# Second attention: the queries of two heads in seven products of blocks, and the groups of one batch element after those of the other

## The chip, the cores and the metric

The kernel runs on one core of a Trainium2 chip. The time is the device time of one execution, in microseconds (us). A run before the change took 2154.76 us, the median of three (2153.85 to 2155.38).

Five engines work side by side, each through its own instructions in order: PE (matrix products; its weight loads are listed apart as PEld), DVE (vector work), ACT (activations and copies), POOL (vector work out of SBUF) and SP, which issues the DMAs.

## The reference, cut to what matters

The program is a chain of six blocks on x of 2 x 512 tokens by 512 features, all in float32. The second one is the attention that the change touches: 32 query heads of 128 features, 8 key heads, so four query heads share one group of keys and values.

```python
q = (hidden_states @ Wq.T).reshape(bsz, q_len, N_HEADS, HEAD_DIM).transpose(0, 2, 1, 3)
...
q = q * cos + _rotate_half(q) * sin
k = k * cos + _rotate_half(k) * sin
...
c_kv = hidden_states @ Wdk.T
k_c = c_kv @ Wupk.T
v = (c_kv @ Wupv.T).reshape(bsz, q_len, KV_HEADS, HEAD_DIM).transpose(0, 2, 1, 3)
...
scores = jnp.einsum('bhqd,bhkd->bhqk', q, k) * scale
scores = jnp.where(causal[None, None], scores, jnp.asarray(-1000000000.0, dt))
attn = jax.nn.softmax(scores, axis=-1)
out = jnp.einsum('bhqk,bhkd->bhqd', attn, v)
...
return out @ Wo.T
```

`hidden_states` is the layernorm of x, and the result is added to x. For one head the query product is 512 tokens x 512 features x 128 outputs.

## The kernel before

**Layout.** `k.xT[b]` holds the normalised x of batch element b, transposed: features on the partitions, four chunks of 128, by 512 tokens (the tokens in an order in which two of the four tiles run backwards). It is a part of the tile `room`, of which two more parts, `k.spare`, take the probabilities of two units in turn. PSUM's eight banks of 512 columns are held for the whole block and handed out in rotation by `k.turn()`.

**Groups and units.** Before, `groups` runs over the 8 groups and inside a group over the two batch elements: 16 pairs (g, b). A unit is one head of one pair: 64 units. The weights of a group (`wq`, `wo`, `wk`, `wupv`, by `load`, L685) are loaded once and serve both elements; `wq` and `wo` are tiles of 1 MB with the tag w8, which has five buffers and is shared with `wdk` and with the weights of `bound`, a side computation on POOL that a later block needs.

**The start.** L693 to L704 make the latents `ckvT` of both elements: four chains of four products each. The layernorm of the second element's tokens (L698) stands between the two.

**The loop** (L821 to L828), written out by hand, sets PE's order; the planner of the framework orders the other engines by its costs and priorities. In step n:
- `queries` of unit n+1 (L753): a chain of four 128x512 products over the four chunks of features into one bank; then `rope` (L706), three DVE operations out of PSUM (the product with the cosine, and two halves with the sine) and one add on POOL.
- `softmax` of unit n (L760): `exponents` (L222) makes the scores of four query tiles, each in four strips of 32 columns of PE, then DVE adds the mask and takes the maxima, and ACT makes the exponentials with their sums; `normalise` (L259) has a reciprocal on DVE and four products on POOL.
- `beside` (L783), by the place j of the unit in its group. j = 0: the fourth output chain of the group before the last. j = 1: `values` of the last group, 64 products on PE (`attend`), with copies by ACT (`gather`). j = 2: `prepare_keys` of the next group, and two output chains of the last. j = 3: `prepare_values` of the next group, with 16 small DMAs (`spread`, L322), and one output chain.
- `turned` of unit n-1 (L273): DVE transposes the probabilities in blocks of 32 for `values`.

At the end of the block (m = 16, L800) stands the layernorm of the first element for the next block.

Of the kernel before, what the change touches and what calls it, by code (L numbers as in the profile page):

```python
# [31 lines left out]
F32 = mybir.dt.float32  # L32
I32 = mybir.dt.int32
AF = mybir.ActivationFunctionType
ALU = mybir.AluOpType
AX = mybir.AxisListType

B, S, D = 2, 512, 512
P = 128
NT = S // P  # L40
KC = D // P
NTILES = B * NT
# [3 lines left out]
class Block:  # L46
# [39 lines left out]
    def masks(self):  # L86
        nc = self.nc


        self.mask = self.const.tile([P, S], F32, tag="mask", name="mask")  # L90
        nc.gpsimd.memset(self.mask, 0.0)
        nc.gpsimd.affine_select(
            out=self.mask, in_=self.mask, compare_op=ALU.is_ge, fill=-1e30, base=S - P,
            pattern=[[-1, S]], channel_multiplier=1,
        )

        self.mask_back = self.const.tile([P, S], F32, tag="mask_back", name="mask_back")
        nc.gpsimd.memset(self.mask_back, 0.0)
        back = self.mask_back[:, :P]
        nc.gpsimd.affine_select(  # L100
            out=back, in_=back, compare_op=ALU.is_ge, fill=-1e30, base=0,
            pattern=[[1, P]], channel_multiplier=-1,
        )


    def load(self, src, shape, tag, bufs=None, dtype=F32, pool=None):
# [564 lines left out]
def attn_gqa(k, a, bound):  # L671


    nc, tc = k.nc, k.tc
    G, J = 8, 4
    with ExitStack() as ctx:
        lp = ctx.enter_context(tc.tile_pool(name="b", bufs=2))
        one = lambda shape, tag: lp.tile(shape, F32, tag=tag, name=tag, bufs=1)
        wdk = k.load(a["b_wdk"], [P, KC, D], "w8", 5)
        tables = {}  # L680
        for n in ("cosq", "sinq", "cosk", "sink"):
            tables[n] = one([P, S], n)
            nc.sync.dma_start(out=tables[n], in_=a["c_b_" + n])

        def load(g):  # L685
            return dict(
                wq=k.load(a["b_wq"][g], [P, KC, J * P], "w8", 5),
                wo=k.load(a["b_wo"][g], [P, J, D], "w8", 5),
                wk=k.load(a["b_wk"][g], [P, KC, P], "w3", 6),
                wupv=k.load(a["b_wupv"][g], [P, KC, P], "w3", 6),  # L690
            )

        w = {0: load(0)}  # L693
        ckvT = []
        for b in range(B):
            if b:
                for t in range(NT, NTILES):
                    k.layernorm(t, k.turn, back=True)  # L698
            ck = one([P, KC, S], f"ckvT{b}")
            for m in range(KC):  # L700
                ps = k.turn()
                k.chain(ps, [(wdk[:, c, bass.ts(m, P)], k.xT[b][:, c]) for c in range(KC)])
                nc.scalar.copy(ck[:, m], ps)
            ckvT.append(ck)  # L704

        def rope(ps, kind, out):  # L706

            cos, sin = tables["cos" + kind], tables["sin" + kind]
            t2 = k.work.tile([P, S], F32, tag="xn", name="t2")
            nc.vector.tensor_tensor(out, ps, cos, ALU.mult)  # L710
            nc.vector.tensor_tensor(t2[0:64], ps[64:128], sin[64:128], ALU.mult)
            nc.vector.tensor_tensor(t2[64:128], ps[0:64], sin[0:64], ALU.mult)  # L712
            nc.gpsimd.tensor_tensor(out, out, t2, ALU.add)  # L713

        keys, vals = {}, {}

        def prepare_keys(g, b):

            ps = k.turn()


            for c in range(KC):
                for n in range(4):
                    strip = slice(32 * n, 32 * n + 32)
                    src = ckvT[b] if n % 2 else k.xT[b]
                    nc.tensor.matmul(
                        ps[strip],
                        w[g]["wk"][:, c, strip],
                        src[:, c],
                        start=(c == 0),  # L730
                        stop=(c == KC - 1),
                    )
            kt = lp.tile([P, S], F32, tag="kT", name="kT", bufs=3)
            rope(ps, "k", kt)
            keys[g, b] = kt

        def prepare_values(g, b):

            ps = k.turn()
            for t in range(NT):  # L740
                k.chain(
                    ps[:, bass.ts(t, P)],
                    [(ckvT[b][:, c, bass.ts(t, P)], w[g]["wupv"][:, c]) for c in range(KC)],
                )
            vt = lp.tile([P, NT, P], F32, tag="v", name="v")
            nc.scalar.copy(vt.rearrange("p t d -> p (t d)"), ps)
            vals[g, b] = lp.tile([P, S // 32, P], F32, tag="vals", name="vals")
            k.spread(vt, vals[g, b])

        qs, ctxs = {}, {}  # L750
        turned = one([P, J * k.WIDE], "turned")

        def queries(u):  # L753
            g, b, j = u
            ps = k.turn()
            k.chain(ps, [(w[g]["wq"][:, c, bass.ts(j, P)], k.xT[b][:, c]) for c in range(KC)])
            q = qs[u] = lp.tile([P, S], F32, tag="q", name="q")
            rope(ps, "q", q)

        def softmax(u):  # L760
            g, b, j = u
            q = qs.pop(u)
            probs = k.other().rearrange("p t s -> p (t s)")
            k.normalise(probs, k.exponents(q, keys[g, b], probs))
            return probs

        def values(g, b):
            banks = [k.turn() for i in range(4)]
            v = vals[g, b]
            k.attend(banks, [(slice(0, P), lambda i, n: v[32 * i : 32 * i + 32, n], turned)])  # L770
            c = ctxs[g, b] = lp.tile([P, J, S], F32, tag="ctxT", name="ctxT", bufs=1)
            k.gather(banks, c, [nc.scalar.copy] * 4)

        def output(g, b, t):
            ps = k.turn()
            c = ctxs[g, b]
            k.chain(ps, [(c[:, i, bass.ts(t, P)], w[g]["wo"][:, i]) for i in range(J)])
            k.add_to_x(b * NT + t, ps)

        groups = [(g, b) for g in range(G) for b in range(B)]  # L780
        units = [(g, b, j) for g, b in groups for j in range(J)]

        def beside(m, j):  # L783


            before = groups[m - 1] if 0 < m <= len(groups) else None
            if before and j == 1:
                values(*before)
            if m < len(groups) and j == 2 and m + 1 < len(groups):
                prepare_keys(*groups[m + 1])  # L790
            if before and j == 2:
                output(*before, 0)
                output(*before, 1)
            if j == 3 and m + 1 < len(groups):
                prepare_values(*groups[m + 1])
            if before and j == 3:
                output(*before, 2)
            if m > 1 and j == 0:
                output(*groups[m - 2], 3)
            if m == len(groups) and j in (1, 2):  # L800

                for t in (2 * j - 2, 2 * j - 1):
                    k.layernorm(t, k.turn)
            if m < len(groups) and groups[m][1] == 1 and j == 1 and groups[m][0] + 1 < G:
                w[groups[m][0] + 1] = load(groups[m][0] + 1)
            for at, n in ((4, "q"), (9, "k")):
                if (m, j) == (at, 2):
                    bound.begin(n)
                if m == at + 1:
                    bound.square(j)  # L810
                if (m, j) == (at + 2, 0):
                    bound.sum()
            if (m, j) == (12, 0):
                bound.end()

        with tc.manual_schedule(engines={mybir.EngineType.PE}):
            prepare_keys(0, 0)
            queries(units[0])
            prepare_values(0, 0)
            probs = {}  # L820
            for n in range(len(units) + J + 1):  # L821
                if n + 1 < len(units):
                    queries(units[n + 1])
                if n < len(units):
                    probs[n] = softmax(units[n])
                beside(*divmod(n, J))
                if n - 1 in probs:
                    k.turned(probs.pop(n - 1), turned, (n - 1) % J)  # L828

# [813 lines left out]
```

## Time and profile before

| what | value | how to read it |
|---|---|---|
| median of the runs | 2154.76 us | three runs |
| the profiled execution | 2156.43 us | its own time |
| span in its trace | 2154.7 us | first to last instruction |
| mean granted PE clock | 0.987 | over the whole span |
| second attention | about 344 to 1180 us | from the first latent's chain to the last group's values |
| DVE query cosine, 128x512 out of PSUM | 692 ns | L710 |
| POOL query add, 128x512 | 1283 ns, x64 | L713 |
| POOL products of `normalise` | 372, 478, 585, 692 ns | 128, 256, 384, 512 columns, L265 |
| load of `wq` or `wo` | 1 MB, 4.8 us from issue to landing | x8 each |
| load of `vals` by `spread` | 64 KB, 2.0 us | x256 |

A row of the profile gives the source line, the engine, the operation, the tiles written and read, the count, the busy time and the mean time of one. "Idle before" is time in which the engine stood still ahead of these instructions, put down to what ended it. A PE record's time is longer than its share of the stream, since records overlap; the distance between starts is what a product costs.

### The profile page before, as it was taken

What the parts mean: (1) busy time and instruction counts of PE and PEld (TensorE: products, weight loads), DVE (VectorE), ACT (ScalarE), POOL (GpSimd) and SP (SyncE); (2) the same over time, 40 slices, a digit from 0 to 9 for tenths busy, and PEclk for the clock granted to TensorE, in tenths of its full rate; (3) what the DMA queues carried; (4) which work ended last, traced back from release to release, by engine and by line L of the source; (5) the groups of instructions that cost most, each with busy time, mean ns of one, the idle gap of its engine ahead of it and who ended that gap; (6) DMA issues with size and microseconds to landing.
All of it is one profiled execution on the core that took longest, in us unless ns stands there. A gap on an engine that the chain in (4) does not pass through costs nothing. (4 is left out here: it accounts for less than half of the span.)

```text
span 2154.7 us, 38870 instructions
## 1 busy us (share of the span) xinstructions
PE 2068.3 (96%) x15116; PEld 1085.4 (50%) x15116; DVE 1281.2 (59%) x3467; ACT 728.8 (34%) x2040; POOL 719.2 (33%) x988
## 2 busy tenths in 40 slices
PE   7999989999999999999999989999999989999988
PEld 3444434555555555555555444545454544554554
DVE  6578752655555555555555557666666674745745
ACT  2455531222222222222222145444545211532531
POOL 1101010423323324223223246555555544215220
PEclk9999999999999999999999999999999999999999
DMA  3000021211121212121110321010101002002001
GB/s 97 16 1 1 20 89 41 68 40 50 40 70 41 68 25 69 26 84 30 46 36 10 126 60 53 21 51 23 49 22 51 1 30 44 2 2 40 1 2 40
DMA packets 65463, 85.35 MB, mean 40 GB/s; under 512 B 13170, under 2 KB 50162, under 8 KB 60660
## 3 DMA queue, kind: packets, MB, share of 16 engines
q1 hardware_dynamic: 64628, 81.69, 12.7%
q8 instruction: 123, 2.02, 0.4%
q10 hardware_dynamic: 640, 1.05, 0.3%
q14 instruction: 72, 0.59, 0.1%
HBM read 58.59 MB, written 2.10 MB: 28 GB/s over the span
## 5 line engine op out<-in xcount | busy, mean ns | idle before, releaser
L254 ACT ACTIVATE room<-room,nmax 128x128 f32<-128x128 f32 (+3 forms) x384 | 211.2, 551 | 507.3 <-DVE nmax L244 506.2
L265 POOL TENSOR_SCALAR room<-room,invs 128x128 f32<-128x128 f32 (+3 forms) x384 | 197.0, 532 | 95.9 <-DVE invs L262 95.9
L713 POOL TENSOR_TENSOR q<-q,t 128x512 f32<-128x512 f32 x64 | 82.1, 1283 | 423.4 <-DVE t L712 423.4
L305 PE MATMUL sc<-turned,vals 32*128 32x256 f32 (+7 forms) x1004 | 187.3, 420 | 0.0
L305 PE MATMUL tp<-turned,vals 32*128 32x384 f32 (+7 forms) x742 | 170.9, 411 | 0.0
L305 PE MATMUL pj<-turned,vals 32*128 32x384 f32 (+7 forms) x754 | 146.8, 416 | 3.1 <-DVE turned L278 3.1
L233 PE MATMUL sc<-kT,q 128*32 128x160 f32 (+15 forms) x1536 | 139.5, 399 | 8.6 <-DVE invs L262 7.9
L278 DVE STREAM_TRANSPOSE turned<-room 128x1152 f32<-128x1152 f32 x80 | 108.0, 1363 | 66.4 <-POOL room L265 22.1
L305 PEld LDWEIGHTS sc<-turned,vals 32*128 32x128 f32 (+1 forms) x1004 | 122.5, 167 | 6.2 <-issue 4.1
L160 PE MATMUL pj<-room,w 128*128 128x512 f32 x272 | 121.1, 595 | 0.2 <-ACT room L191 0.2
L160 PE MATMUL sc<-room,w 128*128 128x512 f32 x232 | 105.4, 597 | 0.2 <-ACT room L191 0.2
L305 PEld LDWEIGHTS tp<-turned,vals 32*128 32x128 f32 (+1 forms) x742 | 102.9, 167 | 5.0 <-issue 2.7
L305 PEld LDWEIGHTS pj<-turned,vals 32*128 32x128 f32 (+1 forms) x754 | 97.8, 169 | 11.8 <-DVE turned L278 5.8
L160 PE MATMUL sc<-w,room 128*128 128x512 f32 (+1 forms) x224 | 100.5, 595 | 0.0
L233 PE MATMUL tp<-kT,q 128*32 128x224 f32 (+15 forms) x1032 | 92.4, 392 | 6.9 <-DVE invs L262 6.9
L201 POOL TENSOR_TENSOR rstd<-ve,mhalf 128x1 f32<-128x1 f32 x80 | 44.1, 554 | 160.8 <-DVE ve L199 137.4
L233 PE MATMUL pj<-kT,q 128*32 128x512 f32 (+4 forms) x992 | 92.7, 407 | 2.9 <-POOL q L993 1.9
L254 ACT ACTIVATE probs<-probs,nmax 128x128 f32<-128x128 f32 (+3 forms) x128 | 71.1, 556 | 65.5 <-DVE nmax L244 64.2
L160 PE MATMUL sc<-w,ctxT 128*128 128x512 f32 x192 | 87.5, 598 | 0.0
L233 PEld LDWEIGHTS sc<-kT,q 128*32 128x32 f32 x1536 | 61.8, 110 | 50.0 <-issue 20.6
L265 POOL TENSOR_SCALAR probs<-probs,invs 128x128 f32<-128x128 f32 (+3 forms) x128 | 65.6, 532 | 61.3 <-DVE invs L262 57.4
L523 PE MATMUL sc<-qm,keys 32*128 32x512 f32 x198 | 85.5, 638 | 0.0
(577 smaller groups left out, 5734.6 us busy)
## 6 DMA issues: line engine op xcount, KB each, us to landing
vals<-v SPq DMA_DIRECT2D x256, 64.0 KB, 2.0
w<-in_b_wq SPq DMA_DIRECT2D x8, 1024.0 KB, 4.8
w<-in_b_wo SPq DMA_DIRECT2D x8, 1024.0 KB, 4.8
w<-in_m_wo SPq DMA_DIRECT2D x8, 1024.0 KB, 6.4
w<-in_f_w SPq DMA_DIRECT2D x4, 1024.0 KB, 4.8
w<-in_m_wqn SPq DMA_DIRECT2D x8, 384.0 KB, 3.2
x<-in_x SPq DMA_DIRECT2D x8, 256.0 KB, 5.1
w<-in_b_wk SPq DMA_DIRECT2D x8, 256.0 KB, 2.6
```

Source lines behind the costliest of these rows:

```text
L160: last = self.nc.tensor.matmul(out, lhsT, rhs, start=(i == 0), stop=(i == len(pairs) - 1))
L201: self.nc.gpsimd.tensor_tensor(r, ve, self.mhalf, ALU.pow)
L233: nc.tensor.matmul(ps[32 * i : 32 * i + 32, a - lo : b - lo], q[:, at : at + 32], keys[:, a:b], start=True, stop=True,)
L254: nc.scalar.activation(row, row, AF.Exp, bias=nmax, scale=-1.0, accum_out=total[:, qt : qt + 1])
L265: self.nc.gpsimd.tensor_scalar(row, row, inv[:, qt : qt + 1], 1.0, ALU.mult, ALU.mult)
L278: self.nc.vector.transpose(out[:, :last], probs[:, :last])
L305: self.nc.tensor.matmul(out[:, :, :n], values(i, j), rhs, start=(j == blocks[0]), stop=(j == stop[i]),)
L523: nc.tensor.matmul(ps, keys[b][rows[g], bass.ts(kc, P)], qm[u][rows[g]], start=True, stop=True)
L713: nc.gpsimd.tensor_tensor(out, out, t2, ALU.add)
```

## The change

**Seven products.** Two heads and the two halves of the features make weight blocks a11, a12 (first head), a21, a22 (second); the halves of the features and of the tokens make the blocks of x. In place of eight products of blocks (each now 128 outputs x 256 tokens, two chunks of features), seven are made, of sums of blocks:
- `token_sums(b)`: four DVE subtractions (128x512 elements), once per batch element.
- `weight_sums(m, i)`: four POOL operations (128x256) for each pair of heads, one of which overwrites a21 in the weight tile.
- `queries(m, i, part)`: part 0 makes two products, which ACT copies out of PSUM; part 1 two more, with two DVE adds and two POOL adds; part 2 the last three, with three DVE adds, then the rotation: two DVE halves with the sine for each head, now out of SBUF, and the product with the cosine and the add on POOL.

In the loop, a pair's parts 0 and 1 stand around the scores of an even unit, and part 2 ahead of the scores of the odd one; they are for the pair of the next two units.

**The order of the groups.** All eight groups of the first element, then all of the second. Each of the 16 groups loads its own `wq`, `wo`, `wk` and `wupv`, and `wdk` is loaded a second time (at m = 5). The second element's layernorm (m = 5) and latents (m = 7, j = 0 and 1) move from the start into the loop, and the first element's layernorm for the next block from the end to m = 13. `ckvT` has one buffer, `kT` two in place of three, `v` one in place of two, `q` three in place of two.

**The masks** of two tiles of 512 columns become two views of one tile of 640.

```diff
         def load(g):
             return dict(
                 wq=k.load(a["b_wq"][g], [P, KC, J * P], "w8", 5),
-                wo=k.load(a["b_wo"][g], [P, J, D], "w8", 5),
...
+        groups = [(g, b) for b in range(B) for g in range(G)]
...
+        tokens = lambda b, c, n: k.xT[b][:, 2 * c : 2 * c + 2, bass.ts(n, S // 2)]
+        heads = lambda m, i, r, c: w[m]["wq"][:, 2 * c : 2 * c + 2, bass.ts(2 * i + r, P)]
+
+        ends = [s.rearrange("p c s -> p (c s)")[:, k.TRIANGLE :] for s in k.spare]
+        xs = [one([P, 2, S // 2], f"x_sum{i}") for i in range(3)]
+        xs.append(ends[1][:, :S].rearrange("p (c s) -> p c s", c=2))
...
+        def token_sums(b):
+            sub = lambda out, x, y: nc.vector.tensor_tensor(out, x, y, ALU.subtract)
+            sub(xs[0], tokens(b, 0, 1), tokens(b, 0, 0))
+            sub(xs[1], tokens(b, 1, 1), xs[0])
+            sub(xs[2], tokens(b, 1, 1), tokens(b, 0, 1))
+            sub(xs[3], tokens(b, 1, 0), xs[1])
+
+        def weight_sums(m, i):
+            op = nc.gpsimd.tensor_tensor
+            s = lp.tile([P, 3, 2, P], F32, tag="wq_sum", name="wq_sum")
+            both, less, last = (s[:, n] for n in range(3))
+            a11, a12, a21, a22 = (heads(m, i, r, c) for r in range(2) for c in range(2))
+            op(both, a21, a22, ALU.add)
+            op(less, both, a11, ALU.subtract)
+            op(last, a12, less, ALU.subtract)
+            op(a21, a11, a21, ALU.subtract)
+            ws[m, i] = a11, a12, a21, a22, both, less, last
+
+        def product(out, lhsT, rhs):
+            for c in range(2):
+                nc.tensor.matmul(out, lhsT[:, c], rhs[:, c], start=c == 0, stop=c == 1)
...
-        def queries(u):
-            g, b, j = u
-            ps = k.turn()
-            k.chain(ps, [(w[g]["wq"][:, c, bass.ts(j, P)], k.xT[b][:, c]) for c in range(KC)])
-            q = qs[u] = lp.tile([P, S], F32, tag="q", name="q")
-            rope(ps, "q", q)
+        def queries(m, i, part):
...
+            if part == 0:
+                ps = k.turn()
+                product(ps[:, first], a11, x(0, 0))
+                product(ps[:, second], both, xs[0])
+                nc.scalar.copy(copies, ps)
+            elif part == 1:
...
+                ps = k.turn()
+                product(ps[:, first], less, xs[1])
+                product(ps[:, second], diff, xs[2])
+                add(q0[:, second], ps[:, first], copies[:, first])
+                add(q1[:, first], ps[:, second], q0[:, second])
+                for out, of in ((q0[:, second], q0[:, second]), (q1[:, second], q1[:, first])):
+                    nc.gpsimd.tensor_tensor(out, of, copies[:, second], ALU.add)
+            else:
...
+                product(ps[:, first], a12, x(1, 0))
+                product(ps[:, second], a22, xs[3])
+                add(q0[:, first], ps[:, first], copies[:, first])
+                add(q1[:, first], ps[:, second], q1[:, first])
+                ps = k.turn()
+                product(ps[:, first], last, x(1, 1))
+                add(q0[:, second], ps[:, first], q0[:, second])
+                for q in pair:
...
+                    nc.vector.tensor_tensor(t2[0:64], q[64:128], sin[64:128], ALU.mult)
+                    nc.vector.tensor_tensor(t2[64:128], q[0:64], sin[0:64], ALU.mult)
+                    nc.gpsimd.tensor_tensor(q, q, tables["cosq"], ALU.mult)
+                    nc.gpsimd.tensor_tensor(q, q, t2, ALU.add)
...
             for n in range(len(units) + J + 1):
-                if n + 1 < len(units):
-                    queries(units[n + 1])
+                m, i = divmod((n + 2) // 2, 2)
+                more = m < len(groups)
+                if more:
+                    queries(m, i, 2 * (n % 2))
                 if n < len(units):
-                    probs[n] = softmax(units[n])
+                    probs[n] = softmax(*units[n])
+                if more and n % 2 == 0:
+                    queries(m, i, 1)
+                if (m, i, n % 2) == (G - 1, 1, 1):
+                    token_sums(1)
                 beside(*divmod(n, J))
+                if n % 2 == 0 and n + 4 < len(units):
+                    weight_sums(*divmod(n // 2 + 2, 2))
                 if n - 1 in probs:
                     k.turned(probs.pop(n - 1), turned, (n - 1) % J)
```

## The prediction

> **What bounds the kernel.** I read the page's busy shares and slices first, then the busy time by windows inside the second attention, then the waits there, then single weight loads on the time line. The page's own chain of waits is short here (PE 7% of the span) and says nothing of this stage.
>
> ```profile
> PE 2068.3 (96%) x15116; PEld 1085.4 (50%) x15116; DVE 1281.2 (59%) x3467; ACT 728.8 (34%) x2040; POOL 719.2 (33%) x988
> ...
> PE   7999989999999999999999989999999989999988
> ...
> POOL 1101010423323324223223246555555544215220
> PEclk9999999999999999999999999999999999999999
> ```
> ```profile
> 600.00:700.00 100.00, 100.00 (x740) 55.16 (x739) 51.76 (x125) 24.10 (x82) 27.27 (x40) 1.00 0.19 56
> 700.00:800.00 100.00, 100.00 (x739) 55.88 (x741) 52.96 (x123) 23.88 (x81) 27.88 (x40) 1.00 0.17 48
> ```
> The windows' columns are PE, PEld, DVE, ACT, POOL, then granted clock. From 380 to 1150 us PE is never idle at a granted clock of 1.00, DVE is at 53%, POOL at 27 to 39%. The stage is bound by PE's stream, so PE work removed there is time removed, as long as nothing else becomes late. The waits of the stage say the same: the long ones are of other engines for PE's products.
>
> ```profile
> ACT room L254 <- DVE nmax L244: 486.7, 61, 13.6
> POOL q L713 <- DVE t L712: 407.0, 61, 9.1
> ```
>
> **PE: the products.** PE's price is read from the starts of the weight loads.
> ```profile
> 382.07 3.54 PEld L160 LDWEIGHTS pj<-w,ckvT 128*128 128x128 f32 x31 [0.24 <-issue]
> 385.53 0.30 PEld L160 LDWEIGHTS tp<-room,w 128*128 128x128 f32 x2
> 386.08 0.19 PEld L160 LDWEIGHTS tp<-room,w 128*128 128x128 f32 x1 [0.24 <-issue]
> 386.51 0.19 PEld L160 LDWEIGHTS tp<-room,w 128*128 128x128 f32 x1 [0.24 <-issue]
> ...
> 388.22 0.19 PEld L160 LDWEIGHTS tp<-room,w 128*128 128x128 f32 x1 [0.24 <-issue]
> 389.17 0.16 PEld L233 LDWEIGHTS sc<-kT,q 128*32 128x32 f32 x8 [0.76 <-issue]
> ```
> Each fp32 matmul of the program is two records (four of a query chain give eight loads). With 512 columns a record takes 0.429 us (386.08 to 386.51). With 128 columns, 32 records take 385.53 - 382.07 = 3.46 us, 0.108 each: a quarter, so even there the loads of 128 weights stay hidden. A record of 256 columns, which the trace lacks, is then 0.214 us (between a half, 0.214, and 0.22 with the small surplus of the 128-column row). Two heads cost 16 x 0.429 = 6.86 us; seven products of two matmuls are 28 records x 0.214 = 6.00. Gain 0.86 us a pair, x32 pairs = **-27.4 us** (-22 with 0.22).
>
> **PE: one more change of tiling per group.** In step j=2 the keys followed the scores at once, both with 32-column weights; now the products of part 1 stand between.
> ```profile
> 540.25 0.53 PEld L233 LDWEIGHTS sc<-kT,q 128*32 128x32 f32 x8
> 540.92 0.11 PEld L726 LDWEIGHTS av<-room,w 128*32 128x32 f32 x1
> ...
> 544.89 0.30 PEld L160 LDWEIGHTS sc<-w,ctxT 128*128 128x128 f32 x2 [0.84 <-ACT room L254]
> 545.42 0.19 PEld L160 LDWEIGHTS sc<-w,ctxT 128*128 128x128 f32 x1 [0.24 <-issue]
> ```
> Into 32-column weights costs 0.09 us (the matmul loaded at 388.22 ends at 389.08, the next load is at 389.17). Out of them costs 0.22: the last keys end at 544.78, the first full matmul starts at 545.42 - 0.43 = 544.99. Together 0.31 x 15 groups with keys after scores = **+4.7 us**. The other steps keep their number of changes.
>
> **DVE and ACT.** Per pair DVE loses two cosine products (0.69 each) and gains five adds of 256 columns from PSUM (no row; nearest, the masked maximum of 128x256, 0.42): 2.1 - 1.4 = +0.7 us in 23 us, on an engine at 53%. ACT gains one copy of 512 columns, 0.59, at 24%. Beside PE, 0. They come ahead of the scores' maxima in DVE's queue, which the next scores' banks wait for: eight banks in rotation are about 11 us of PE work, so that cover is wide.
>
> **POOL** takes most. A two-input 128x512 takes 1.28 us; 256 columns I estimate at 0.7 (half, plus part of a fixed cost of about 0.27, from the scaling rows 0.48 at 256 and 0.69 at 512). Per group of four heads: sums of weights 8 x 0.7 = 5.6, part 1's adds 4 x 0.7 = 2.8, cosine product and last add 8 x 1.28 = 10.2, key 1.27, normalising 4 x 2.06 = 8.2: 28 us, against 14.6 before, in a group of about 48.8 us (780 us from 380 to 1160, 16 groups) that becomes 47.3. POOL goes from 30% to 60%. Throughput is free; latency is what can cost. In POOL's order each pair runs: normalise unit 2p, part 1's adds, (key,) sums for a later pair, cosine and add for q0, then q1, normalise 2p+1. So q0 of the next pair waits for the scores of 2p: their start to the end of normalising was 7.3 us (389.2 to 396.5; 5.6 if the rope is not ahead of the maxima), then 1.4 + 1.3 + 2.8 + 2.6 = 8.1, together at most 15.4 us. Until scores 2p+2, PE has from j=0 to j=2: scores 2.0, part 1 1.7, output 3.4, part 2 2.6, scores 2.0, values 7.5, part 0 1.7 = 20.9; from j=2 to j=0: 27. Slack 5 us or more: 0.
>
> Here the Trainium skill speaks against the change: *GPSIMD Engine Reference*, Specifications, says GpSimd shares its SBUF interfaces with VectorE and contends with VectorE instructions that have two SBUF inputs. The rotation's sine products read q from SBUF now, not PSUM: exactly that kind. The trace has the case later, in the last attention:
> ```profile
> L1304 DVE TENSOR_TENSOR t<-t,w x16: 691/834/1210, 1779.2 to 1961.2; 128x512 f32<-128x512 f32 x16
> L1305 POOL TENSOR_TENSOR room<-room,w x16: 1261/1740/1783, 1779.2 to 1963.3; 128x512 f32<-128x512 f32 x16
> ```
> (minimum/median/maximum ns.) Ignoring the rule, the chain is 15.4; with all of its 8.1 us of two-input POOL work at 1.74/1.28, 18.4, and DVE's four sines 0.5 longer each. Still inside 20.9. The row decides: contention is real, but hidden in the steady state.
>
> **The first group** has no values and no outputs: PE has 2 x 6.0 + 4 x 2.0 + 3.5 (keys) + 3.5 (values) = 27 us against POOL's 28. Between scores 0 and scores 2 PE has only 2.0 + 1.7 + 2.6 + 2.0 + 1.7 = 10.0; the chain is 5.6 to 7.3, plus 8.1: q0 late by 3.7 to 5.4 us; I take the lower end, since the next rope no longer stands ahead of these maxima. Scores 4 and 6 have 16.9 and more. Before, this group ran without a gap. **+3.7 us** (0 to 10).
>
> **What else moves.** The second element's layernorm leaves the start (PE waited 0.84 for xn and 0.84 for its copy: -1 us), the first one's leaves the end, where PE waited 2.7 us for the last transposes on DVE, behind its work (-0.5 only: scores, maxima and exponentials make them late anyway). The token sums are eight DVE operations of 0.7 us, hidden behind keys and values. Loads: wq, wo and the two small ones come 16 times in place of 8, +20 MB on 16 queues with a busy share of 0.17 to 0.19; each lands in 4.8 us and is issued a group ahead in SP's order, save where the bound's weight or wdk holds a buffer of w8: there it waits for the output of two groups back and lands inside the 12 us of step j=1. POOL would stand at the sums; +1 us, up to 5. The mask tile's memset and selects lie in the first stage, off PE: 0.
>
> **Sum:** -27.4 + 4.7 + 3.7 - 1.5 + 1 = **-19.5 us**. The profiled execution took 2156.4 us (span 2154.7), 1.7 above the median of 2154.76; the same difference off the median gives **2135.3 us**.
>
> **Rivals.**
> 1. *Only the stream counts* (chance 0.17): no late q0, and part 1 costs no change of tiling: -27.4 - 1.5, 2126. For it: PE's perfect cover. Against: the switch is in the trace.
> 2. *Partial stalls* (0.14): loads or sums late in the groups with a borrowed buffer, or q0 late after j=0 by half a us in each group: +8, so 2143. For it: the third attention, with POOL at 62%, shows PE idle 20.5 of 412 us, a part of it waiting for q from POOL and for the reciprocal.
> 3. *POOL's chain becomes the bound* (0.07), the other side. It needs the chain j=0 to j=2 over 20.9 us; each us beyond costs 15. It breaks even at 20.9 + 19.5/15 = 22.2, so POOL's 8.1 would have to become 14.9, 1.84 times. At twice the price (16.2, with 7.3 ahead, 23.5): 2.6 x 15 = 39 us, 2174. The measured ratio is 1.36.
> 4. *Nothing visible* (0.04): gain and stalls cancel, 2155.
> The forecast has the rest, 0.58, with its own range 2130 to 2141.
>
> **Chances and range.** A change under 0.2% (4.3 us) can't be told from none. Faster: forecast, rivals 1 and 2, less what of 2 grows past 15 us: 0.87. Same 0.06, slower 0.07. The range holds the forecast, rival 1 with its bounds (gain 22 to 27, switch 0 to 5) and most of 2: 2124 to 2149.
>
> **What would show it.** Product records of 256 columns 0.214 us apart; PE idle 3 to 5 us before scores 2 and nowhere else in the stage; POOL at 55 to 65%, its sums and cosines 1.3 to 1.7 us; DVE's sines up to 1.2. Regular PE gaps ahead of the even units' scores, released by POOL's q, would make me wrong, as would records nearer 0.25.

## The result and the profile after

The changed kernel takes **2145.18 us** (median of 6 runs, 2143.77 to 2146.52) where the kernel before takes 2154.71 (2152.46 to 2155.38) beside it: ratio 0.9957, 95% interval 0.9944 to 0.9970. That is 9.5 us faster, with 19.5 forecast; 2145.2 lies inside the range of 2124 to 2149 and outside the forecast's own 2130 to 2141.

The page of the changed kernel, busy time by engine and the slices that answer to those shown before:

```profile
span 2143.5 us, 40021 instructions
...
PE 2048.5 (96%) x15500; PEld 1147.2 (54%) x15500; DVE 1349.5 (63%) x3571; ACT 749.0 (35%) x2072; POOL 972.9 (45%) x1243
...
PE   6999989899999999999999989999999989999988
...
POOL 1101023767665557666762256555555544215220
PEclk9999999899999999999999999999999999999999
```

PE lost 20 us of busy time against 2068.3, the span only 11.2 against 2154.7. In PEclk the eighth digit is an 8: something happens near 375 to 430 us. Busy time by windows in the steady part of the second attention, in the columns of the prediction (length of the window, PE, PEld, DVE, ACT, POOL, then granted clock, DMA share, GB/s):

```profile
600.00:700.00 100.00, 100.00 (x808) 64.82 (x807) 64.58 (x142) 28.70 (x90) 60.12 (x74) 1.00 0.25 75
700.00:800.00 100.00, 100.00 (x765) 64.22 (x767) 56.88 (x127) 26.94 (x82) 57.91 (x68) 1.00 0.26 83
```

POOL went from 27 to 60 of 100 us and DVE from 53 to 61, and PE still never stands: the steady part is as forecast. The start is not. The same columns, for the first group and the beginning of the second:

```profile
340.00:380.00 40.00, 37.24 (x181) 21.74 (x180) 14.61 (x31) 7.00 (x15) 13.74 (x13) 0.96 0.26 84
380.00:400.00 20.00, 15.88 (x127) 9.28 (x125) 15.19 (x36) 5.69 (x19) 17.59 (x23) 0.91 0.22 71
400.00:430.00 30.00, 27.24 (x209) 20.30 (x209) 21.21 (x45) 6.14 (x20) 23.29 (x27) 0.89 0.30 89
```

PE is idle for 9.6 of these 90 us, and its clock is below 1.00 in all three. The time line of PE names the places (start, duration, then in brackets the idle time before and who ended it):

```profile
374.94 0.36 PE L229 MATMUL sc<-kT,q 128*32 128x32 f32 x5 [2.08 <-POOL q L832]
...
391.21 0.32 PE L229 MATMUL tp<-kT,q 128*32 128x32 f32 x5 [4.12 <-POOL q L832]
...
411.33 0.32 PE L229 MATMUL sc<-kT,q 128*32 128x32 f32 x5 [0.69 <-POOL q L832]
...
424.05 1.21 PE L301 MATMUL tp<-turned,vals 32*128 32x512 f32 x1 [2.08 <-DVE q L798]
```

Scores 0, 2 and 4 wait for POOL's last add of the rotation, and a product of values(0) waits for a PSUM bank that DVE has not yet emptied. The second was forecast (3.7 us), the other three were not. **And here each wait of 2 us or more has a slow stretch at its end.** The 32 records of scores take 1.97 us in the steady part; here scores 0 took 3.66 and scores 2 took 2.93. values(0), 7.56 us in the steady part, took 14.73, of which 2.08 are the wait. The sum over the segments from scores 0 to values(0), each against the same segment in the steady part, is +17.5 us: 9.0 of waits, 8.5 of slow PE.

Why q is late shows on POOL's time line between scores 0 (at 374.94) and scores 2 (at 391.21):

```profile
380.61 2.05 POOL L261 TENSOR_SCALAR room<-room,invs 128x128 f32<-128x128 f32 x4 [3.14 <-DVE invs L258]
382.63 1.42 POOL L815 TENSOR_TENSOR q<-q,room 128x256 f32<-128x256 f32 x2
384.00 0.73 POOL L781 TENSOR_TENSOR wq_sum<-w 128x256 f32<-128x256 f32 x1
...
387.77 1.71 POOL L831 TENSOR_TENSOR q<-q,cosq 128x512 f32<-128x512 f32 x1
389.56 1.60 POOL L832 TENSOR_TENSOR q<-q,t 128x512 f32<-128x512 f32 x1
```

L261 normalises head 0, L815 are part 1's two adds, L781 begins the sums of the weights, L831 and L832 are cosine product and last add. So q of head 2 comes after the whole softmax of head 0, 16.2 us after its scores, where PE had 12.1 us of other work. Part 1's adds do not need that softmax; they stand behind its normalising only because of the order. On DVE the same knot is tied twice:

```profile
380.33 0.18 DVE L258 RECIPROCAL invs<-total 128x4 f32<-128x4 f32 x1 [0.88 <-ACT room L250]
380.64 0.43 DVE L798 TENSOR_TENSOR q<-tp,room 128x256 f32<-128x256 f32 x1
...
382.70 1.38 DVE L274 STREAM_TRANSPOSE turned<-room 128x1152 f32<-128x1152 f32 x1 [1.06 <-POOL room L261]
384.00 0.39 DVE L798 TENSOR_TENSOR q<-sc,room 128x256 f32<-128x256 f32 x1
...
388.37 1.65 DVE L830 TENSOR_TENSOR t<-q,sinq 64x512 f32<-64x512 f32 x1
```

Part 1's first add (380.64) waited behind the maxima and the reciprocal, and part 2's adds (from 384.00) behind a transpose that itself waits for the normalising.

### The profile page after: what moved, and what is told of

It is laid out like the page before. It is cut to its first block, busy times and chain, and to the rows that moved or that the text cites. A ratio compares the mean times of both kernels' runs of the same rounds, so it can differ in the third digit from the quotient of the medians.

```text
span 2143.5 us, 40021 instructions
## 1 busy us (share of the span) xinstructions
PE 2048.5 (96%) x15500; PEld 1147.2 (54%) x15500; DVE 1349.5 (63%) x3571; ACT 749.0 (35%) x2072; POOL 972.9 (45%) x1243
## 5 line engine op out<-in xcount | busy, mean ns | idle before, releaser
L261 POOL TENSOR_SCALAR room<-room,invs 128x128 f32<-128x128 f32 (+3 forms) x384 | 197.5, 534 | 144.9 <-DVE invs L258 144.9
L301 PE MATMUL sc<-turned,vals 32*128 32x128 f32 (+7 forms) x1090 | 188.4, 424 | 0.0
L229 PE MATMUL sc<-kT,q 128*32 128x256 f32 (+3 forms) x1496 | 135.8, 398 | 11.4 <-DVE invs L258 7.9
L301 PE MATMUL pj<-turned,vals 32*128 32x256 f32 (+7 forms) x602 | 126.1, 424 | 1.3 <-DVE turned L274 1.3
L831 POOL TENSOR_TENSOR q<-q,cosq 128x512 f32<-128x512 f32 x64 | 95.4, 1491 | 60.0 <-DVE t L830 60.0
L229 PE MATMUL tp<-kT,q 128*32 128x32 f32 (+15 forms) x1072 | 98.6, 401 | 11.2 <-DVE invs L258 7.1
L229 PE MATMUL pj<-kT,q 128*32 128x96 f32 (+15 forms) x1048 | 100.5, 417 | 2.9 <-POOL q L1096 1.9
L301 PE MATMUL av<-turned,vals 32*128 32x384 f32 (+7 forms) x372 | 99.9, 419 | 0.0
L156 PE MATMUL sc<-w,ctxT 128*128 128x512 f32 x208 | 94.2, 595 | 0.0
L261 POOL TENSOR_SCALAR probs<-probs,invs 128x128 f32<-128x128 f32 (+3 forms) x128 | 65.6, 532 | 60.6 <-DVE invs L258 56.7
L832 POOL TENSOR_TENSOR q<-q,t 128x512 f32<-128x512 f32 x64 | 87.5, 1367 | 4.3
L1093 POOL TENSOR_TENSOR t<-t,sinq 128x512 f32<-128x512 f32 x32 | 40.9, 1277 | 106.1 <-DVE invs L258 101.3
L273 DVE STREAM_TRANSPOSE turned<-room 128x128 f32<-128x128 f32 x80 | 24.4, 305 | 101.0 <-POOL room L261 100.9
```

The source lines that it names most:

```text
L156: last = self.nc.tensor.matmul(out, lhsT, rhs, start=(i == 0), stop=(i == len(pairs) - 1))
L229: nc.tensor.matmul(ps[32 * i : 32 * i + 32, a - lo : b - lo], q[:, at : at + 32], keys[:, a:b], start=True, stop=True,)
L261: self.nc.gpsimd.tensor_scalar(row, row, inv[:, qt : qt + 1], 1.0, ALU.mult, ALU.mult)
L273: self.nc.vector.transpose(out[:, self.WIDE - P :], probs[:, last : last + P])
L301: self.nc.tensor.matmul(out[:, :, :n], values(i, j), rhs, start=(j == blocks[0]), stop=(j == stop[i]),)
L831: nc.gpsimd.tensor_tensor(q, q, tables["cosq"], ALU.mult)
```

## The experiments

A "plain group" below is the time from the first product of one values step to that of the next, in groups without a layernorm, latents or bound: 50.95 us before, 49.39 after. It repeats to 0.01 us, so one profile settles what a change does to the steady part, where medians scatter by 2 or 3 us. "Waits" are PE's gaps of over 0.3 us from 345 to 430 us. "values(15)" is the start of the stage's last values step on the profile's time line (1173.1 before the change): what an edit does to the stage. Behind it no edit changes anything, and yet the profiles need 979 to 982 us from there to the end in some kernels and 984 to 986 in e2_two, e5_keys, e9_early, e9_dve and e9_two. In the first four of these five the third attention ran at a clock of 0.90 to 0.93 between 1200 and 1300 us, against 0.98 in the changed kernel; why is open.

| kernel | median us | ratio to before, 95% | plain group | waits | values(15) at |
|---|---|---|---|---|---|
| changed kernel | 2145.18 | 0.9957 (0.9944 to 0.9970) | 49.39 | 9.0 | 1164.1 |
| e3_order | 2151.19 | 0.9988 (0.9981 to 0.9994) | 50.95 | 0 | 1171.5 |
| e1_first | 2136.39 | 0.9917 (0.9902 to 0.9932) | 49.39 | 3.7 | 1155.0 |
| e2_two | 2133.33 | 0.9899 (0.9883 to 0.9916) | 49.39 | 0 | 1147.9 |
| e4_fill | 2148.34 | 0.9974 (0.9966 to 0.9981) | 49.39 | 5.0 | 1162.6 |
| e5_keys | 2132.18 | 0.9895 (0.9864 to 0.9925) | 49.06 | 0 | 1142.9 |
| e7_dve | 2142.39 | 0.9934 (0.9913 to 0.9955) | 49.39 | 9.5 | 1160.7 |
| e9_early | 2133.42 | 0.9891 (0.9874 to 0.9907) | 49.06 | 5.1 | 1148.2 |
| e9_dve | 2133.80 | 0.9894 (0.9878 to 0.9911) | 49.06 | 5.7 | 1148.8 |
| e9_first | 2128.35 | 0.9884 (0.9866 to 0.9902) | 49.06 | 2.6 | 1146.2 |
| e9_two | 2130.43 | 0.9878 (0.9861 to 0.9894) | 49.06 | 0 | 1145.4 |

**Is it the start, the steady part or the order?** Three kernels take the seven products back, for the first group, for the first two, and for all (the last then needs no sums of tokens).

```
+        def plain(m, j):
+            ps = k.turn()
+            k.chain(ps, [(w[m]["wq"][:, c, bass.ts(j, P)], k.xT[b][:, c]) for c in range(KC)])
+            q = qs[m, j] = lp.tile([P, S], F32, tag="q", name="q", bufs=3)
+            rope(ps, "q", q)
         def queries(m, i, part):
+            if m == 0:              # e2_two: m < 2;  e3_order: always
+                if part != 1:
+                    plain(m, 2 * i + part // 2)
+                return
```

> The changed kernel, with the four heads of the first group alone made as before the change (eight products, rotation out of PSUM, no sums of blocks). Theory A (the loss lies in the first two groups: PE waits for q from POOL, and the granted clock falls after each wait): the waits ahead of scores 0, 2 and 4 (2.1 + 4.1 + 0.7 us) go, and some 3.5 us of reduced clock with them; two pairs pay 0.86 us again, less one change of tiling: 2145.2 - 6.9 - 3.5 + 1.4 = 2136. Rival B (the loss is spread over all groups, by contention of DVE and POOL and by changes of tiling): two pairs of 32 change nothing but their own price: 2145 to 2147. Rival C (the new order of the groups and its loads cost the time): 2145 to 2147 too.

> As the one before, with the first two groups (eight heads) made as before the change. Theory A: the third wait goes too (2.1 us ahead of a product of values(0), whose bank waits for DVE's add, which waits for POOL's) with about 2 us of reduced clock behind it, for 1.4 us more of products: 2136 - 2.1 - 2 + 1.4 = 2133. If the third wait has gone with the first two already: 2137. Rivals B and C: 2147 to 2148.

> The new order of the groups, the later layernorms and the doubled loads, with eight products for all heads and no sums of blocks: what the order alone does. Theory A: next to nothing, 2153 to 2155 (layernorm out of the way -1.5, loads +1), with PE idle under 1 us from 345 us to 430 us. Rival C: it costs what is missing, 2160 to 2165. Rival B says nothing of it.

Measured 2136.4, 2133.3 and 2151.2: theory A to within a us for the first two, and 2 us under its 2153 for the third. With one group put back, the waits before scores 0 and 2 are gone; left are 1.64 us before scores 4 and the 2.08 in values(0). With two groups back no wait is left there. The waits of PE from 340 to 1200 us, first with one group put back, then with two (0.8 and 0.7, in both, lie outside 345 to 1150 us):

```profile
PE pj L301 <- DVE q L809: 2.1, 1, 2.1
PE pj L229 <- POOL q L843: 1.6, 1, 1.6
PE pj L646 <- ACT ctxT L316: 0.8, 1, 0.8
PE sc L156 <- ACT room L187: 0.7, 1, 0.7
```
```profile
PE tp L646 <- ACT ctxT L316: 0.8, 1, 0.8
PE sc L156 <- ACT room L187: 0.7, 1, 0.7
```

(Columns: who waited for whom, us in total, times, longest.) The third wait alone is worth 7.3 us, not 2.1: from values(0) to values(1) the kernel with one group put back needs 56.89 us, the one with two 49.63. So the 2133 that the expectation had, with 4 us for this wait, was met by luck: in the profiles e2_two is 7.1 us ahead of e1_first at values(15), and 4.8 of them are lost behind it. The order alone gives -3 us and no wait, so it costs nothing (rival C falls), and 49.39 against its 50.95 in every plain group leaves nothing for rival B.

**Does the idle time lower the clock, and is that the price?** Products that nobody reads stand where PE waited.

```
             a11, a12, diff, a22, both, less, last = ws[m, i]
+            fill = {(0, 1, 0): 5, (1, 0, 0): 9, (1, 1, 2): 5}.get((m, i, part))
+            if fill:
+                ps = k.turn()
+                for n in range(fill):
+                    nc.tensor.matmul(ps[:, : S // 2], a12[:, 0], tokens(b, 1, 0)[:, 0], start=True, stop=True)
```

> The changed kernel with products that nobody reads in PE's three waits, each group of them in a bank of its own: 5 matmuls of 256 columns (2.1 us) ahead of scores 0, 9 (3.9 us) ahead of scores 2, 5 (2.1 us) ahead of values(0). PE is busy where it stood before; the output is the same. If the idle stretches are what lowers the granted clock (theory A), the clock stays at 1.00 and only the slow stretch behind each wait goes: 2145.2 - 5 = 2140. If the clock falls for another reason, the time stays at 2145, or gets longer by what the filling overlaps badly.

A miss, and a useful one: 2148.3, 3 us longer than without the filling. The same windows as above, of this kernel:

```profile
340.00:380.00 40.00, 39.33 (x198) 24.32 (x197) 15.84 (x35) 7.24 (x17) 14.66 (x16) 1.00 0.27 83
380.00:400.00 20.00, 19.74 (x154) 12.85 (x152) 13.52 (x32) 5.16 (x17) 15.53 (x20) 1.00 0.28 85
400.00:430.00 30.00, 25.02 (x224) 19.38 (x227) 20.71 (x42) 6.15 (x20) 23.37 (x27) 0.94 0.28 80
```

The clock stays at 1.00 where it was 0.96 and 0.91: the idle stretches had lowered it. But at the next gate most of that was lost:

```profile
412.50 0.32 PE L229 MATMUL tp<-kT,q 128*32 128x32 f32 x5 [4.99 <-POOL q L837]
```

Scores 4 began at 412.50, against 411.33 in the changed kernel, though PE came there earlier. Up to scores 4 the first group is bound by the making of q, not by PE, whatever clock PE has; the slow stretches of the first two waits were covered by the wait that would have stood at scores 4. Only the one in values(0) is paid in full: from values(0) to values(1) this kernel needs 50.16 us, the changed one 56.57. Ahead of that it loses 5.0 us: 1.2 at scores 4, 1.6 of reduced clock behind their wait, 2.2 of the last filling itself. So it gained 1.4 us in the stage where 5 were expected, and the 3 us of the medians arise behind the stage; their cause is open.

**POOL's own work, or the way through the softmax?** First the weight sums of the first two groups on DVE, POOL 4.2 us a pair shorter:

```
-            op = nc.gpsimd.tensor_tensor
+            op = (nc.vector if m < 2 else nc.gpsimd).tensor_tensor
```

> The changed kernel, seven products for all heads, with the sums of the weights of the first two groups (four operations of 256 columns a pair) on DVE in place of POOL. Theory A (POOL's chain of some 20 us from one pair's scores to the next pair's q is longer than PE's cover in the first group): the chain is 4.2 us shorter and DVE some 1.7 us longer, so the waits before scores 2 and 4 shrink from 4.1 and 0.7 to under 1.6 us, the one in values(0) goes, and no stretch of reduced clock is left behind them: 2133 to 2137. Rival (the chain's length comes from the maxima, the exponentials and DVE, not from POOL's own work): the waits stay within 1 us of 2.1, 4.1 and 2.1 or grow, 2143 to 2149.

2142.4, with waits of 0.8, 5.1, 1.1 and 2.5 us: no wait went except most of the first, which is nearer to the rival. From scores 0 to q of head 2 it took 15.5 us (16.2), from scores 2 to q of head 4 20.3 (20.1). POOL stood where the sums had been, because the cosine product overwrites q and so has to wait for DVE's sines:

```profile
381.18 1.42 POOL L815 TENSOR_TENSOR q<-q,room 128x256 f32<-128x256 f32 x2
385.31 1.76 POOL L831 TENSOR_TENSOR q<-q,cosq 128x512 f32<-128x512 f32 x1 [2.71 <-DVE t L830]
387.15 1.59 POOL L832 TENSOR_TENSOR q<-q,t 128x512 f32<-128x512 f32 x1
```

So the chain goes through both engines in turn. The edit does not separate the two accounts cleanly, since it made DVE's part longer as well: three of the four sums took 1.4 to 1.5 us each on DVE, where 1.7 were expected for all four, and head 0's first maximum stood behind them, 3.0 us after the start of its scores (0.6 in the changed kernel). The next edit takes q's first half out of the softmax's way, with all heads on seven products:

```
+                if more and n % 2 == 0:
+                    queries(m, i, 1)
                 if n < len(units):
                     probs[n] = softmax(*units[n])
-                if more and n % 2 == 0:
-                    queries(m, i, 1)
```

> The changed kernel with part 1 of a pair's products ahead of the even head's scores on PE, right behind part 0. On DVE the first of its two adds comes ahead of the scores' maxima, and on POOL its two adds come ahead of the normalising of that head. Theory A' (q's chain runs through the softmax of the head before: maxima, reciprocal, normalising, and only then part 1's adds, DVE's adds and sines, cosine, last add): the chain loses 1.4 us on POOL at least and up to 4 us where DVE's sines were what POOL waited for, so the waits before scores 2 and 4 and in values(0) shrink from 6.9 us together to 1 to 5, with less reduced clock; and a plain group loses a change of tiling, 49.39 - 0.33 = 49.06 us. Together 2145.2 - 4.9 - 2 to 8: 2132 to 2138. Rival (POOL's throughput alone bounds the first group: its work is the same here): only the tiling, 2140, with waits of 6 us or more.

2133.4, waits of 0.4, 3.4 and 1.3 us, plain group 49.06. No wait is left in values(0), but the last of the three, in scores 5, is again one for a bank that DVE's add has to empty. POOL's time line, from q of head 1 to q of head 2:

```profile
376.23 1.41 POOL L815 TENSOR_TENSOR q<-q,room 128x256 f32<-128x256 f32 x2 [0.20 <-ACT room L250]
378.11 2.52 POOL L261 TENSOR_SCALAR room<-room,invs 128x128 f32<-128x128 f32 x4 [0.47 <-DVE invs L258]
...
384.67 1.27 POOL L831 TENSOR_TENSOR q<-q,cosq 128x512 f32<-128x512 f32 x1
386.02 1.26 POOL L832 TENSOR_TENSOR q<-q,t 128x512 f32<-128x512 f32 x1
```

Part 1's adds now stand ahead of the normalising, and q of head 2 comes 13.8 us after scores 0 (16.2 before the edit), that of head 4 17.9 after scores 2 (20.1). From 374 to 408 us POOL now waits for others for only 2.1 us: what is left before scores 2 is mostly its own work.

> The one before with the weight sums of the first two groups on DVE. With part 1's adds out of the softmax's way, POOL's 4.2 us of sums are what is left between the normalising and the cosine product; taking them away should let q come 2 to 3 us earlier before scores 2, if DVE is then not what POOL waits for: 0 to 4 us under the kernel with part 1 early. If DVE's sines are the tail of the chain, as they were with the sums moved alone, within 1 us of it or over it.

2133.8, no difference: the waits became 1.8, 1.4 and 2.5 us. The one before scores 2 lost 1.6 of its 3.4 us, so POOL's sums were a part of it, but the others grew. DVE now carries the sums in the same chain: they end at 376.9, DVE's first add of part 1 stands behind them, and POOL's adds wait 2.1 us for DVE, up to 378.78.

**What the change of tiling costs.** With the first two groups as before the change (no waits), the keys go ahead of part 1:

```
+                if n % J == 2 and n // J + 1 < len(groups):
+                    prepare_keys(n // J + 1)
                 if more and n % 2 == 0:
                     queries(m, i, 1)
```

> The first two groups as before the change, and in step j=2 the keys of the next group right behind the scores, part 1 of the products behind them: one change of tiling less in each group, the order of the work on the other engines otherwise kept. If a change of tiling costs the 0.31 us of the prediction, a plain group of the stage takes 49.39 - 0.31 = 49.08 us and the kernel 2133.3 - 4.5 = 2129. If the two weight loads hide behind the stream (the products account for 1.63 of the 1.56 us that a group gained, which leaves 0.07 for the change of tiling), 49.3 us and 2132 to 2133. If part 1, now 3.6 us later, makes q late: over 49.4 us, with PE idle before the scores of j=0.

Plain groups of 49.06 us, so 0.33 for the change of tiling, as the prediction priced it (0.31); the medians, 2132.2 and 2133.3, can't show it. The account "0.07 is left" was wrong because it took the products' gain from their columns alone and left out 0.24 us a group that the values step gains (next section).

**How near is POOL to being the bound?** On the kernel with two groups put back, sums made again ahead of the cosine product:

```
-            op(both, a21, a22, ALU.add)
+            for n in range(4 if m > 2 else 1):      # e8_pool7: 8
+                op(both, a21, a22, ALU.add)
```

> The kernel with its first two groups as before the change, and three more sums of 256 columns (a sum of weights made again, same value) on POOL for each pair from the fourth group on, ahead of the pair's cosine product: 2.2 to 3.5 us more of POOL's chain. q is ready 3.5 to 6 us ahead of the scores in the steady groups of the changed kernel's trace. If that slack is real, nothing is seen: a group stays at 49.39 us, the kernel at 2133, with q 1 to 3 us ahead. If POOL's throughput or contention with DVE already costs something, groups grow by more than 0.3 us each.

> As the one before, with seven more sums in place of three: 5.1 to 8.2 us more in the chain, over the slack of 3.5 to 6. From q's slack: each pair's scores late by 1 to 3 us, 26 pairs, so a group 52 to 55 us in place of 49.4 and the kernel 2133 + 35 to 60, more where the waits lower the granted clock. If POOL's chain is not what stands next to PE: under 5 us.

One run each: 2145.99 and 2211.71, where 2133 and 2168 to 2193 were expected: two misses on the slow side. From values(0) to values(15) they need 751.5 and 819.0 us against 737.3, so +14 and +82. The waits of the first, from 420 to 1160 us:

```profile
PE sc L791 <- POOL wq_sum L783: 3.6, 3, 2.4
PE tp L791 <- POOL wq_sum L783: 2.6, 2, 2.3
PE pj L156 <- DVE x L205: 1.9, 1, 1.9
PE av L229 <- DVE t L715: 0.7, 1, 0.7
```

These are 8.8 of the 14 us; where the rest lies was not followed. Mostly it is not q that is late but the sums: at 521, 676 and 890 us, in groups where POOL makes the sums of two pairs one behind the other, just ahead of part 0. In five groups, which take at most 0.34 us more than in the changed kernel, the slack holds. That the late groups are those where the bound's weight or wdk has a buffer of w8, so that the weights come late, fits their numbers; it was not tested.

**Together.** Part 1 early, with the first group, or the first two, as before the change:

> Part 1 early in all groups but the first, whose four heads are made as before the change. No wait is left before scores 0 and 2; the third, in values(0), goes too if part 1's adds no longer stand behind the normalising: plain groups of 49.06 us, PE idle under 1.5 us from 345 to 1150 us, 2136.4 - 4.6 - 3 = 2128 to 2130 us. If the third wait stays: 2131 to 2133.

> Part 1 early, the first two groups as before the change: no wait at all and 49.06 us a plain group, 2133.3 - 13 x 0.33 = 2129, 1.6 us above the same with one group, if that one has no wait.

2128.35 and 2130.43, with one wait of 2.6 us (in scores 5, for DVE's add) and with none. So the third wait of the first expectation stayed, and its 2128 to 2130 for the case without it was met by luck. The intervals of their ratios, 0.9866 to 0.9902 and 0.9861 to 0.9894, do not part the two; both beat the kernel before and the changed one.

## Why the prediction was wrong, and what in it was right

- **Products, -27.4.** Records of 256 columns come 0.216 us apart, as forecast (0.214). Against the kernel with the new order alone, the product steps of a plain group take 12.87 us in place of 14.21 with the change of tiling in them, and values, followed by a narrower product, 7.56 in place of 7.80. With the change of tiling taken out (49.06 against 50.95) that is -1.89 a group, -30 in all: 1.65 of the products (1.71 forecast) and the 0.24 of values, which the forecast lacked.
- **Change of tiling, +4.7.** 0.33 a group, +5.
- **Order, layernorms and loads, -0.5.** -3.0, -1.3 to -4.1 us by the interval of the ratio. Its waits of 0.84, 0.84 and 2.7 us are waits of the weight loads (PEld): PE itself stood for 0.24 us from 340 to 380 us and 1.9 ahead of the last values step. In the profiles 1.6 us were gained up to values(15) and 2.4 behind it.
- **Steady POOL and DVE, 0.** Right: no wait from 430 to 1150 us. The first q of a pair comes 3.5 to 6 us ahead of its scores in the groups of the trace (forecast: 5 or more). For the cosine product contention was of the size that the row of the last attention gave, 1.27 to 1.77 us; sums took 0.73 alone and up to 1.18, sines 0.69 alone and up to 1.67 (1.2 forecast). Here the *GPSIMD Engine Reference* of the Trainium skill, Specifications, names the right pair of engines, and the cover of the steady groups hid what it costs; the first group did not.
- **First group, +3.7: the step that failed.** It measured +17.5. The prediction expected one late q there, before scores 2, and took PE's cover at scores 0, at scores 4 and in values(0) for enough. The lines of POOL and DVE at the three places that it missed:

```profile
367.64 0.73 POOL L781 TENSOR_TENSOR wq_sum<-w 128x256 f32<-128x256 f32 x1
...
373.63 1.26 POOL L832 TENSOR_TENSOR q<-q,t 128x512 f32<-128x512 f32 x1
...
402.87 1.29 POOL L716 TENSOR_TENSOR kT<-kT,t 128x512 f32<-128x512 f32 x1 [2.09 <-DVE t L715]
...
420.12 2.05 POOL L261 TENSOR_SCALAR room<-room,invs 128x128 f32<-128x128 f32 x4 [4.23 <-DVE invs L258]
422.14 1.40 POOL L815 TENSOR_TENSOR q<-q,room 128x256 f32<-128x256 f32 x2
423.57 0.42 DVE L798 TENSOR_TENSOR q<-tp,q 128x256 f32<-128x256 f32 x1 [2.44 <-POOL q L815]
```

- *Scores 0.* The first pair's q stands in POOL's order behind the sums of the next pair's weights, 4.2 us from 367.64 on, and its last add ends at 374.89: 2.1 us of waiting, 0.8 with those sums on DVE.
- *Scores 2.* The wait came where it was forecast (4.1 us), but its size is in part luck. The 8.1 us behind the normalising hold 1.3 for a key, and no key stands there; against the 12.4 us that are left the chain took 16.2. It needed 7.7 in place of 5.6 up to the end of the normalising (the scores themselves ran 1.7 slow), 3.8 in place of 2.8 for the sums and 3.4 in place of 2.6 for cosine and add, whose long rows (1.17 to 1.71 us) lie beside DVE's sines. PE's cover was 12.1 in place of 10.0, mostly by the same slow scores.
- *Scores 4.* "Scores 4 and 6 have 16.9 and more" was held against a chain of 15.4, but from scores 2 to q of head 4 it is 20.1 us. The key's own 1.3 was counted; not counted were 2.1 us of POOL's waiting for DVE ahead of it, 1.3 more for the sums, 0.5 more for cosine and add, and 0.9 up to the normalising. 0.7 us of that showed.
- *values(0).* The sentence "eight banks in rotation are about 11 us of PE work, so that cover is wide" overlooked that values takes four banks at once, while part 2's bank waits for DVE, DVE for part 1's adds on POOL, and these for the normalising: 2.1 us in the second group. That later groups are spared because they have an output step at j=0 fits, and was not tested.
- **The granted clock** was not in the sum at all. 8.5 of the 17.5 us are what PE lost at half speed; 5.1 of them, in values(0), are certainly paid, the rest lies in the stretch that POOL bounds anyway.

Sum of the measured terms: -30.2 + 5.0 - 3.0 + 17.5 = -10.7, for 9.5 us measured. Of the rivals, the second (waits of +8) came nearest in time, but with its waits in the wrong place: it had them in every group. The third was priced too low: at five to eight us more of POOL's work it gives +82, not break-even, since the sums are late too (PE waits 31.5 us for them, in five places) and the clock falls at each of the five.

## What to carry to other kernels

When work moves to an engine that shares a chain with another, follow one result through the in-order queues of all engines, at the start of the loop as well as in its steady part: the first turns lack the work that covers the chain later. Where a value waits behind a step that it doesn't depend on (here part 1's adds behind a softmax), moving it ahead can be worth more than handing work to another engine of the same chain: one moved call gave 12 us, 5 of them by its change of tiling, and 4.2 us a pair handed from POOL to DVE in two groups gave 3. A wait of PE can cost more than its length (2.1 us in values(0) cost 7.2), but only where PE sets the time afterwards.

## What the runs showed of the hardware

PE's clock after idle time. The granted clock by windows of the changed kernel, around the wait in values(0) (421.97 to 424.05):

```profile
396.00:422.00 26.00, 25.29 (x208) 16.22 (x206) 17.66 (x39) 5.64 (x18) 18.10 (x23) 1.00 0.21 56
422.00:430.00 8.00, 5.95 (x33) 5.40 (x37) 6.30 (x11) 0.49 (x2) 7.84 (x9) 0.57 0.43 149
430.00:432.00 2.00, 2.00 (x32) 1.85 (x29) 1.11 (x5) 1.91 (x6) 1.92 (x3) 1.00 0.00 0
```

It falls to 0.50 around the end of a wait, stays there for 3 to 7 us and comes back. In the start of the stage, in the changed kernel and six of the experiments, this followed nine of ten waits of 2.1 us or more (2.1 three times, 2.5, 2.6, 3.4, 4.1, 5.0, 5.1), with one of 2.5 left out, and none of those from 0.7 to 1.8 us. A longer wait did not mean a longer slow stretch: after 4.1 us it lasted 3.4, after the 2.1 in values(0) 6.8.

The length of the wait alone does not decide, though. In the steady part of e8_pool3 two waits of 2.3 us left the clock at 1.00, and so did one of 2.7 in the third attention of e9_two; in that of e5_keys it stood at 0.50 for 17 us from 1230 on, with no single wait over 0.8 us in the 20 us before. The Trainium skill, *TensorE: Matmul & The Clock Gate*, Part 1, has half rate after an idle window of some 3.4 us whose start runs free, and full rate after about as long a busy one. The half rate and the length of the slow stretches in the stage's start (3.4 or 6.8 us) agree with that; that a single gap of 2.1 us could be enough, three times out of three there, does not, and the measurement decides. What else has a part in it these runs do not show.
